# Two transformer layers on one core: one of eight band distances taken from the tokens' difference, and five smaller edits

## The chip, the cores and the metric

The kernel runs on one core of one Trainium2 chip, as one launch. The core has four engines that compute: TensorE (PE; its weight loads are listed apart as PEld), VectorE (DVE), ScalarE (ACT) and GpSimd (POOL). SyncE (SP) issues most of the DMAs. Each engine takes its own queue in order; they meet through semaphores. The metric is the device time of a launch in microseconds (us), the median of several runs, lower is better. Beside it there is one execution taken by the hardware profiler, and all durations below are from that one.

## The reference

Input x has shape (4, 512, 128): four rows of 512 tokens with 128 channels, all in float32. Each of two layers computes `xn = layernorm(x)` and `x = x + attention(xn) + experts(xn)`. Cut to what matters:

```python
# layer 0, attention: 16 heads, 16 displacement channels each, window of 64 tokens
disp = heads(xn @ W_disp); val = heads(xn @ W_val)            # (B, 16, T, 16), (B, 16, T, 8)
strain = windows(disp, 64) - disp[:, :, :, None, :]           # token t-63 .. t, minus token t
bond   = gelu(strain @ W_strain + rel_pos_emb @ W_pos) @ W_bond
damage = sigmoid(gelu(strain @ W_dmg + b_dmg) @ W_dmg_out + b_dmg_out)
weights = softmax(where(causal, bond - 10.0 * damage, -inf))  # over the 64
attention0 = concat(einsum(weights, windows(val, 64))) @ W_cproj
# layer 0, experts: t = rmsnorm(xn) * scale; top 4 of 16 by gate, softmax of their scores, swiglu experts
# layer 1, attention: 16 heads of 8, softmax over all 512 tokens, no mask
# layer 1, experts: router relu(xn @ rw1 + rb1) @ rw2 + rb2, top 2 of 8, softmax of the two,
#                   experts relu(xn @ W1 + b1) @ W2 + b2
```

Strain is linear in the tokens: `(disp[t-d] - disp[t]) @ W_strain` is the same as `(xn[t-d] - xn[t])` projected with `W_disp` and `W_strain` merged. At distance d = 0 the strain is zero for every token.

## The kernel before

**Layer 0** (lines 690 to 994) goes over the four rows. `prepare(b)` normalises a row (`layernorm`, lines 210 to 236: statistics of four tiles, one Sqrt on ScalarE, four normalisations), transposes it to `xnT`, and multiplies it with `merged` (displacement and bond or damage weights in one matrix of 128 x 128 for each of two kinds and two halves of the heads) into `proj` (lines 739 and 740). It also makes the values `valn` and the experts' gate through `routes`.

`band_logits(b)` makes the logits of the 64 distances. A distance is `8 * do + 4 * dq + dd` with do in 0..7, dq in 0..1 and dd in 0..3. For every do, for both kinds (1 is damage, 0 is bond), and for every dd there is one tile `z` of 128 partitions with both dq and both head halves, some 4 x 480 elements: VectorE subtracts two shifted views of `proj` (line 790), ScalarE applies Gelu in place (line 792 for damage in one operation; line 796 for bond in two, since the bias depends on the distance), and TensorE multiplies each quarter with a placing matrix of 32 columns into one of four column strips of a PSUM bank (line 804). Four `z` buffers rotate. Four dd make a bank full, and a Tanh (damage, line 819) or three VectorE operations (bond, lines 822 to 827) read it. After all do, the maxima over the window are subtracted, Exp is applied (line 850, tile `e`) and the row is stored to DRAM (`by_t`, line 851).

Beside this, `gated_experts(b)` runs the row's 16 experts (lines 901 to 923; its PSUM tiles `gbank` come from a pool of three banks), `band_values(b - 1)` multiplies the row before's weights with the values: it loads `f` from `by_t` (line 317), transposes it (line 326), stores it to `by_s` (line 332), loads it back skewed as `wb` (line 344) and multiplies (lines 358 and 362). `begin(b - 1)` then normalises that row for layer 1 and computes its router. `weave` interleaves these generators' steps in the shares that stand beside them.

**Layer 1** (from line 997) weaves `full_attention` (142 steps; products of scores on line 1205, maxima on VectorE on line 1222, Exp on ScalarE on line 1229, weighted values on line 1117) with a second track: the last row's band values, its `begin`, its expert order (`row3`), `experts` for the pairs of the first three rows (`first_experts`) and of the last one, and `results`. An expert block is one weight load `wx` and one gather of rows `xb` by GpSimd (line 581), a turn (lines 604 and 606), a first product (line 637) with Relu (lines 648 and 650), a second one (line 611), and a store of `y` to `ys` (line 619). `results` gathers each token's two rows of `ys` back (`got`, line 581 again) and adds them to x (line 676), `lag` steps after the gather.

What sets the order: each engine's queue is fixed when the program is built. The tile framework's scheduler puts the woven steps in order by priority and by its own estimates of readiness; the placing matmuls, the scores, the maxima and the Exps are raised in priority. `paced` and `behind` tie the experts' products and the results to the steps that are already issued. Where a function (`exp`, `tanh`, `gelu`, `sqrt`) is not in the table that ScalarE holds, a table load goes before it; `Relu` and copies need none.

## Time and profile before

| | us |
|---|---|
| median of three runs | 1317.91 |
| lowest and highest | 1314.45 and 1323.61 |
| the profiled execution's own time | 1310.25 |
| its span, first to last instruction | 1308.1 |

| engine | busy us | share of the span |
|---|---|---|
| TensorE | 1027.7 | 79% |
| VectorE | 1010.7 | 77% |
| ScalarE | 955.3 | 73% |
| GpSimd | 139.1 | 11% |

The shares are averages over two layers of different kind. Layer 0 ends at about 838 us, layer 1 takes the rest. The mean granted clock of TensorE is 0.903 of full speed. A row of busy times gives, for each stretch of time, the busy microseconds of each engine. A row of a group gives the source line, engine, operation, the tiles written and read, the number of instructions, then busy time and the mean of one in ns, then the engine's idle time just before them and what ended it. A line in order of time gives start and duration, and in brackets the idle time before it with its releaser.

### The profile page before, as it was taken

The page shows a single profiled execution, that of the slowest core. Times are in us where ns is not written, and L with a number is a line of the kernel's source. Part 1 is how long each engine was busy: PE and PEld are TensorE (multiplying, and loading weights), DVE is VectorE, ACT ScalarE, POOL GpSimd, SP SyncE. Part 2 cuts the span into 40 slices and gives each one's busy share as a digit, 9 for nine tenths or more (in the row PEclk, how much of TensorE's full clock was granted, in tenths as well). Part 3 has the DMA queues.
Part 4 walks back from the last instruction along what each step waited for, and adds up shares of the span by engine and source line. Part 5 has one row for each costly group of instructions (what it writes and reads, how often), then busy time and mean ns, then how long its engine had stood idle before and what let it go on. Part 6 is the DMA issues. An engine that isn't in the chain of part 4 may idle for free. (4 is left out here: it accounts for less than half of the span.)

```text
span 1308.1 us, 18393 instructions
## 1 busy us (share of the span) xinstructions
PE 1027.7 (79%) x7029; PEld 463.6 (35%) x7029; DVE 1010.7 (77%) x1246; ACT 955.3 (73%) x1154; POOL 139.1 (11%) x165
## 2 busy tenths in 40 slices
PE   5677876778796677897577886739898999978996
PEld 3232333223342132443222342414344545534442
DVE  5999999999988999998999979625355475545552
ACT  5999998999987899898899987224454445534454
POOL 3000000000000000000000000231121123234512
PEclk9898898889998799898788988759999999989999
DMA  7221213347212445311355411154632324532431
GB/s 272 65 85 43 73 55 131 84 117 181 57 46 79 116 105 144 99 57 32 123 131 143 122 51 29 63 164 124 169 93 94 97 66 123 144 104 90 122 112 37
DMA packets 161969, 132.17 MB, mean 101 GB/s; under 512 B 68101, under 2 KB 142266, under 8 KB 160346
## 3 DMA queue, kind: packets, MB, share of 16 engines
q1 hardware_dynamic: 151290, 91.72, 25.7%
q0 software_dynamic: 10304, 38.64, 9.5%
q8 instruction: 56, 0.92, 0.3%
q10 hardware_dynamic: 288, 0.64, 0.1%
q14 instruction: 31, 0.25, 0.1%
HBM read 97.93 MB, written 33.03 MB: 100 GB/s over the span
## 5 line engine op out<-in xcount | busy, mean ns | idle before, releaser
L790 DVE TENSOR_TENSOR z<-proj 128x2044 f32<-128x2044 f32 (+31 forms) x256 | 547.8, 2161 | 14.3 <-PE lbank L804 10.1
L804 PE MATMUL lbank<-z,place 128*32 128x504 f32 (+18 forms) x2048 | 302.5, 669 | 135.2 <-ACT z L796 73.4
L796 ACT ACTIVATE z<-z,posb 128x1024 f32<-128x1024 f32 (+31 forms) x256 | 264.3, 1100 | 24.3 <-DVE z L790 23.6
L792 ACT ACTIVATE z<-z,brep 128x2048 f32<-128x2048 f32 (+31 forms) x128 | 240.8, 1913 | 13.7 <-DVE z L790 11.2
L1229 ACT ACTIVATE ex<-score 128x1024 f32<-128x1024 f32 x128 | 130.4, 1024 | 160.7 <-PE score L1205 160.7
L1222 DVE TENSOR_REDUCE nmax<-score 128x2 f32<-128x1024 f32 x128 | 156.1, 1224 | 84.6 <-PE score L1205 84.2
L804 PEld LDWEIGHTS lbank<-z,place 128*32 128x32 f32 x2048 | 45.3, 115 | 288.9 <-ACT z L796 150.7
L1205 PE MATMUL score<-kpad,qpad 32*128 32x512 f32 x384 | 111.4, 652 | 19.4 <-DVE nmax L1222 14.1
L581 POOL DMA_INDIRECT wx<-pair_weights,which x46 | 43.5, 946 | 663.9 <-PE abank L1097 432.4
L1205 PE MATMUL score<-qa,kpad 32*128 32x512 f32 x384 | 104.1, 654 | 2.9 <-ACT ex L1229 2.8
L893 PE MATMUL accbank<-wT,lin 128*128 128x128 f32 x512 | 84.8, 308 | 23.7 <-DVE lin L891 23.6
L893 PEld LDWEIGHTS accbank<-wT,lin 128*128 128x128 f32 x512 | 71.9, 210 | 75.3 <-DVE lin L891 39.1
L906 PE MATMUL gbank<-tT,wT 128*128 128x512 f32 x128 | 73.3, 656 | 27.1 <-DMA wT<-wT_all 21.2
L648 DVE TENSOR_SCALAR h<-bank,wx 128x128 f32<-128x128 f32 x46 | 16.0, 349 | 77.9 <-ACT h L650 77.9
L913 PE MATMUL gbank<-tT,wT 128*128 128x512 f32 x128 | 69.3, 624 | 4.5 <-ACT glu L909 4.5
L1117 PE MATMUL accbank<-ex,vaug 128*32 128x512 f32 x512 | 71.1, 621 | 0.2 <-ACT ex L1229 0.2
L650 ACT ACTIVATE h<-bank,wx 128x128 f32<-128x128 f32 x138 | 40.7, 365 | 39.2 <-PE bank L637 39.1
L637 PE MATMUL bank<-xbT,wx 128*128 128x128 f32 x368 | 53.9, 291 | 4.3 <-DVE y L618 3.5
L637 PEld LDWEIGHTS bank<-xbT,wx 128*128 128x128 f32 x368 | 47.4, 201 | 24.3 <-issue 15.1
L611 PEld LDWEIGHTS bank<-wx,h 128*128 128x128 f32 x368 | 46.6, 197 | 21.5 <-issue 19.0
L611 PE MATMUL bank<-wx,h 128*128 128x128 f32 x368 | 53.4, 289 | 0.8 <-ACT g L327 0.6
L909 ACT ACTIVATE glu<-gbank,gbt 128x512 f32<-128x512 f32 x64 | 44.2, 690 | 9.0 <-PE gbank L906 6.4
(242 smaller groups left out, 1379.8 us busy)
## 6 DMA issues: line engine op xcount, KB each, us to landing
r<-route SPq DMA_DIRECT2D x64, 256.0 KB
wb<-by_s SPq DMA_DIRECT2D x32, 512.0 KB
wT<-wT_all SPq DMA_DIRECT2D x48, 192.0 KB
by_t<-e SPq DMA_DIRECT2D x8, 1024.0 KB
f<-by_t SPq DMA_DIRECT2D x128, 64.0 KB
by_s<-g SPq DMA_DIRECT2D x16, 512.0 KB
wb<-by_s SPq DMA_DIRECT2D x24, 256.0 KB
by_s<-zero POOLq DMA_DIRECT2D x4, 1024.0 KB, 11.0
```

The source lines that it names most:

```text
L611: mm = nc.tensor.matmul(py[:, 0:C], h[:, c * P:(c + 1) * P], wx[j][:, F1 + c * P:F1 + (c + 1) * P], start=(c == 0), stop=(c == 3),)
L637: mm = nc.tensor.matmul(ph[:, c * P:(c + 1) * P], wx[j][:, c * P:(c + 1) * P], xbT[g][:, j % 2 * P:(j % 2 + 1) * P], start=True, stop=True,)
L790: nc.vector.tensor_tensor(z[:, :, :, 0:n], seen, own, ALU.subtract)
L792: nc.scalar.activation(z[:, :, :, 0:n], z[:, :, :, 0:n], AF.Gelu, bias=b_dmg)
L796: last = nc.scalar.activation(z[:, dq, :, 0:n], z[:, dq, :, 0:n], AF.Gelu, bias=posb[:, j:j + 1])
L804: mm = nc.tensor.matmul(ps[q:q + 32, t0:T], place[:, kind, 3 - dd:35 - dd], z[:, dq, hg, 0:n], start=(dd == 0), stop=(dd == 3),)
L893: nc.tensor.matmul(ya[:, i * P:(i + 1) * P], lin[:, i * P:(i + 1) * P], wT[:, 2, :], start=False, stop=(e == E0 - 1 and i == TPB - 1),)
L906: nc.tensor.matmul(pg, wT[:, 0, :], tT, start=True, stop=True)
L1117: mm = nc.tensor.matmul(av[n][r:r + 32, :], vaug[b % 2][:, i, g * 4 + h, :], ex[n, i][:, h, :], start=(i == 0), stop=(i == TPB - 1),)
L1205: mm = nc.tensor.matmul(ps[:, h - two, :], own[r, i * P:(i + 1) * P], seen[r, :], start=True, stop=True)
L1222: freed.append(nc.vector.tensor_reduce(nmax[n % 2][:, i, two:two + 2, 8:9], ps, AX.X, ALU.max, negate=True))
L1229: freed.append(nc.scalar.activation(ex[n, i][:, two:two + 2, :], ps, AF.Exp, scale=inv))
```

## The change

Six edits:

1. *One of eight distances projected.* For dd = 0 and do over 0, the half of `z` with dq = 0 (distance 8 * do) is no longer a difference of `proj`. VectorE makes `xd`, the difference of the tokens themselves (once, used for both kinds), TensorE multiplies it with `merged` for both head halves into two `gbank` tiles in PSUM, and ScalarE's Gelu reads these and writes `z`. The half with dq = 1 is a difference as before, half as large. `tokens[b]` keeps `xnT`, which now has two buffers.
2. *Distance 0.* Its Gelu has the same value for every token: `alike` holds it for each kind, one column, and the placing matmul reads that column repeated.
3. *Routers' exps.* `exp(x)` is computed as `(1 + tanh(x/2)) / (1 - tanh(x/2))`, with three more small VectorE operations.
4. *Statistics.* `layernorm` is split into `statistics` and `normalise_row`; rows 1 to 3 of layer 0 take their statistics together, with one Sqrt.
5. *Band values.* The last row's first step (its loads of `f`) is issued before layer 1's weave, and eight steps of the first experts go ahead of the rest of that track.
6. *Results.* Those of the first three rows have a lag of 3 in place of 2, and five steps of the last experts go ahead of them. Shares of the weave are set to match.

```diff
-    def layernorm(b, dst, pin=False, rms=False):
+    def statistics(lo, n, pin=False, rms=False):
...
+        return mv, rs
+
+    def normalise_row(b, dst, mv, rs):
...
-        nc.scalar.activation(dst, dst, AF.Exp)
-        nc.vector.tensor_tensor(dst, dst, rank, ALU.mult)
+        nc.scalar.activation(dst, dst, AF.Tanh, scale=0.5)
+        below = small.tile([P, TPB, n], FP, tag=f"below{n}", name="below")
+        nc.vector.tensor_scalar(below, dst, -1.0, 1.0, ALU.mult, ALU.add)
+        nc.vector.reciprocal(below, below)
+        nc.vector.scalar_tensor_tensor(dst, dst, 1.0, rank, ALU.add, ALU.mult)
+        nc.vector.tensor_tensor(dst, dst, below, ALU.mult)
...
+            if b < 2:
+
+                stats.append(statistics(b * TPB, NT - TPB if b else TPB, b > 0, True))
+            mv, rs = stats[-1]
...
-            xnT = prep.tile([C, T], FP, tag="xnT", name="xnT")
+            xnT = prep.tile([C, T], FP, tag="xnT", name="xnT", bufs=2)
...
+                        far = slice(0 if dd else 1, 2)
...
-                        nc.vector.tensor_tensor(z[:, :, :, 0:n], seen, own, ALU.subtract)
+                        if dd:
+                            nc.vector.tensor_tensor(z[:, :, :, 0:n], seen, own, ALU.subtract)
+                        else:
+                            if kind and t0:
+                                xd = ap_.tile([C, T], FP, tag="xd", name="xd", bufs=1)
+                                nc.vector.tensor_tensor(
+                                    xd[:, 0:n], tokens[b][:, 0:n], tokens[b][:, t0:T], ALU.subtract
+                                )
+                            nc.vector.tensor_tensor(
+                                z[:, 1, :, 0:n], proj[:, kind, :, 0:n], proj[:, kind, :, 4 + t0:4 + T], ALU.subtract
+                            )
+                        if not dd and t0:
+                            j = WIN - 1 - t0
+                            for hg in range(2):
+                                pz = ps_g.tile([P, T], FP, tag="g", name="gbank")
+                                nc.tensor.matmul(
+                                    pz[:, 0:n], merged[:, kind, hg, :], xd[:, 0:n], start=True, stop=True
+                                )
+                                nc.scalar.activation(
+                                    z[:, 0, hg, 0:n], pz[:, 0:n], AF.Gelu, bias=b_dmg if kind else posb[:, j:j + 1]
+                                )
                         if kind:
-                            nc.scalar.activation(z[:, :, :, 0:n], z[:, :, :, 0:n], AF.Gelu, bias=b_dmg)
+                            nc.scalar.activation(z[:, far, :, 0:n], z[:, far, :, 0:n], AF.Gelu, bias=b_dmg)
                         else:
-                            for dq in range(2):
+                            for dq in range(far.start, 2):
...
-                                        ps[q:q + 32, t0:T], place[:, kind, 3 - dd:35 - dd], z[:, dq, hg, 0:n],
+                                        ps[q:q + 32, t0:T], place[:, kind, 3 - dd:35 - dd],
+                                        z[:, dq, hg, 0:n] if t0 or dq else alike[:, kind:kind + 1].to_broadcast([P, T]),
...
-    first_experts = experts(early, pq, 3)
...
+    first_experts, last_experts = experts(early, pq, 3), experts(last_row, pq, 3)
+    next(row3)
     weave(
         (full_attention(), 142),
         (after(
-            woven((row3, 32), (first_experts, 36)), first_experts,
-            woven((results(early, 2), 9), (experts(last_row, pq, 3), 34)), results(last_row, 1),
-        ), 32 + 66 + 9 + 34 + 3 + 10),
+            some(first_experts, 8), woven((row3, 31), (first_experts, 30)), first_experts,
+            some(last_experts, 5), woven((results(early, 3), 9), (last_experts, 29)), results(last_row, 1),
+        ), 8 + 61 + 28 + 5 + 38 + 3 + 14),
     )
```

`some(g, n)` takes n steps of a generator.

More of the change, by code (lines that the diff above doesn't have):

```diff
@@ L207, in two_layers @@
     b_dmg = brep[:, 34:35]
-    def layernorm(b, dst, pin=False, rms=False):
-        mv = small.tile([P, TPB, 2], FP, tag="mv", name="mv")
-        for i in range(TPB):
+    def statistics(lo, n, pin=False, rms=False):
+        mv = small.tile([P, n, 2], FP, tag=f"mv{n}", name="mv")
+        for i in range(n):
             st = small.tile([P, 6], FP, tag="st", name="st")
-            ins = nc.vector.bn_stats(st, x1[:, b * TPB + i, :])
+            ins = nc.vector.bn_stats(st, x1[:, lo + i, :])
             if pin and not i:
@@ L220, in layernorm @@
         var = mv[:, :, 1]
-        n = 1 + rms
-        sq = small.tile([P, n, TPB], FP, tag=f"sq{n}", name="sq")
+        sq = small.tile([P, 1 + rms, n], FP, tag=f"sq{n * (1 + rms)}", name="sq")
         nc.vector.tensor_scalar(sq[:, 0], var, EPS, None, ALU.add)
@@ L228, in layernorm @@
         nc.scalar.activation(sq, sq, AF.Sqrt)
-        rs = small.tile([P, n, TPB], FP, tag=f"rs{n}", name="rs")
+        rs = small.tile([P, 1 + rms, n], FP, tag=f"rs{n * (1 + rms)}", name="rs")
         nc.vector.reciprocal(rs, sq)
+        return mv, rs
+    def normalise_row(b, dst, mv, rs):
         for i in range(TPB):
             nc.vector.tensor_scalar(
-                dst[:, i, :], x1[:, b * TPB + i, :], mv[:, i, 0:1], rs[:, 0, i:i + 1],
+                dst[:, i, :], x1[:, b * TPB + i, :], mv[:, i, 0:1], rs[:, i:i + 1],
                 ALU.subtract, ALU.mult,
             )
-        return rs[:, n - 1]
     def transposed(src):
@@ L440, in begin @@
         nc.sync.dma_start(out=rw1, in_=w["L1_ffn_rw1"])
-        layernorm(b, xn)
+        mv, rs = statistics(b * TPB, TPB)
+        normalise_row(b, xn, mv, rs[:, 0])
         nc.sync.dma_start(
@@ L687, in after, with some @@
             yield from p
+    def some(g, n):
+        for _ in range(n):
+            next(g)
+            yield
     with ExitStack() as l0:
@@ L722, in two_layers @@
         nc.scalar.copy(merged.rearrange("p k g n -> p (k g n)"), pm)
-        ready = {}
+        ready, tokens = {}, {}
+        stats = []
         def prepare(b):
             xn = prep.tile([P, TPB, C], FP, tag="xn", name="xn")
-            rr = layernorm(b, xn, b > 0, True)
+            if b < 2:
+                stats.append(statistics(b * TPB, NT - TPB if b else TPB, b > 0, True))
+            mv, rs = stats[-1]
+            own = slice((b - 1) * TPB, b * TPB) if b else slice(0, TPB)
+            normalise_row(b, xn, mv[:, own], rs[:, 0, own])
+            rr = rs[:, 1, own]
             pt = transposed(xn)
-            xnT = prep.tile([C, T], FP, tag="xnT", name="xnT")
+            xnT = prep.tile([C, T], FP, tag="xnT", name="xnT", bufs=2)
             nc.scalar.copy(xnT, pt)
@@ L741, in prepare @@
             ready[b] = [proj]
+            tokens[b] = xnT
             yield
@@ L927, in two_layers @@
             next(preparation)
+        alike = keep.tile([P, 2], FP, name="alike")
+        nc.scalar.activation(alike[:, 1:2], b_dmg, AF.Gelu)
         w_posrep = keep.tile([BD, 8, BD], FP, name="w_posrep")
@@ L938, in two_layers @@
         nc.scalar.copy(posb, pst[:, 0:WIN])
+        nc.scalar.activation(alike[:, 0:1], posb[:, WIN - 1:WIN], AF.Gelu)
         half_b_out = keep.tile([P, 1], FP, name="half_b_out")
@@ L1234, in two_layers @@
     pq = ctx1.enter_context(tc.tile_pool(name="experts", bufs=1))
-    first_experts = experts(early, pq, 3)
-    row3 = after(band_values(B - 1, ready[B - 1][1]), begin(B - 1, chain, "valn"), in_order_of_experts(last_row, pq, pq, "tb"))
+    row3 = after(
+        band_values(B - 1, ready[B - 1][1]), begin(B - 1, chain, "valn"), in_order_of_experts(last_row, pq, pq, "tb")
+    )
+    first_experts, last_experts = experts(early, pq, 3), experts(last_row, pq, 3)
+    next(row3)
     weave(
```

## The prediction

> **What bounds the kernel now.** The profiled execution took 1310.25 us (span 1308.1 us). Busy time by stretches comes first: which engine is full, and where. Columns: stretch, length, busy us (instructions) of PE, PEld, DVE, ACT, POOL, granted TensorE clock, DMA share, GB/s.
>
> ```profile
> 16.50:838.00 821.50, 622.43 (x4094) 257.06 (x4092) 767.87 (x827) 736.33 (x796) 0.22 (x2) 0.89 0.33 91
> 838.00:868.00 30.00, 7.91 (x38) 4.29 (x39) 10.27 (x14) 7.33 (x7) 16.54 (x15) 0.69 0.48 166
> 900.00:1284.00 384.00, 348.38 (x2628) 179.27 (x2632) 202.83 (x340) 188.87 (x314) 98.46 (x104) 0.96 0.40 112
> ...
> 225.00:275.00 50.00, 35.16 (x232) 10.94 (x236) 49.74 (x36) 46.78 (x42) 0.00 (x0) 0.80 0.41 108
> 275.00:325.00 50.00, 39.02 (x410) 17.64 (x405) 49.80 (x42) 47.44 (x52) 0.00 (x0) 0.97 0.61 154
> 325.00:375.00 50.00, 42.00 (x240) 16.71 (x232) 49.28 (x77) 49.21 (x59) 0.00 (x0) 1.00 0.22 60
> 375.00:425.00 50.00, 36.01 (x210) 17.31 (x202) 40.80 (x57) 39.94 (x44) 0.11 (x1) 0.84 0.19 63
> ```
>
> Layer 0, to 838 us, is held by VectorE (767.87 of 821.5), with ScalarE close behind (736.33). The last four lines are one batch row. Its first half has VectorE at 99.54 of 100 us, ScalarE at 94.22. In the second half both are near 90 and TensorE is at 78: there the three wait for each other. Then comes a hole (TensorE 7.91 of 30), then layer 1, which TensorE holds (348 of 384). The costliest groups, per operation:
>
> ```profile
> L790 DVE TENSOR_TENSOR z<-proj 128x2044 f32<-128x2044 f32 (+31 forms) x256 | 547.8, 2161 | 14.3 <-PE lbank L804 10.1 <-ACT proj L740 4.1
> L796 ACT ACTIVATE z<-z,posb 128x1024 f32<-128x1024 f32 (+31 forms) x256 | 264.3, 1100 | 24.3 <-DVE z L790 23.6 <-issue 0.2
> L792 ACT ACTIVATE z<-z,brep 128x2048 f32<-128x2048 f32 (+31 forms) x128 | 240.8, 1913 | 13.7 <-DVE z L790 11.2 <-DVE logits L823 2.1
> L819 ACT ACTIVATE dmg<-lbank,half_b_out 128x512 f32<-128x512 f32 (+7 forms) x32 | 21.2, 663 | 9.8 <-PE lbank L804 9.7
> L827 DVE TENSOR_TENSOR mx<-mx,logits 128x504 f32<-128x504 f32 (+6 forms) x28 | 18.2, 651 | 0.1
> L739 PE MATMUL bank<-xnT,merged 128*128 128x512 f32 x32 | 17.9, 685 | 0.7 <-ACT xnT L732 0.7
> ```
>
> L739 has 16 products in the program and 32 in the trace: each fp32 product is two passes, so it costs 17.9/16 = 1.12 us, not 0.685. Last, the order in time at the hole and at the first gathered results:
>
> ```profile
> 867.09 1.94 PE L326 MATMUL bank<-cst,f 128*128 128x128 f32 x8 [16.84 <-DMA f<-by_t]
> ...
> 1166.38 0.35 DVE L676 SCALAR_TENSOR_TENSOR x<-got,gate,x 128x128 f32<-128x128 f32 x1 [5.83 <-DMA got<-ys,place]
> ...
> 1169.25 1.22 PE L1205 MATMUL score<-kpad,qpad 32*128 32x512 f32 x2 [6.82 <-DVE nmax L1222]
> ...
> 1174.52 0.70 PE L1205 MATMUL score<-kpad,qpad 32*128 32x512 f32 x2
> ```
>
> TensorE's queue stood 16.84 us behind a transpose of the last row's band, although other work was ready. Later one VectorE add waited 5.83 us for gathered rows, the maxima behind it came late, TensorE idled 6.82 us, and then a pass took 1.22 us instead of 0.70.
>
> **Projected distance (dd = 0, seven of eight groups, four rows: 28 times, both kinds).** VectorE: L827 (0.651 us at some 484 elements) and L790 (2.161 at some 1922) give 1.05 ns an element, so 1.15 us for 960 and 0.65 for the tokens' difference. Two full differences (4.32) become 2 x 1.15 + 0.65 = 2.95: -1.37 x 28 = -38. ScalarE: the damage kind's 1.91 becomes 1.10 + 2 x 0.66 (L819 also reads PSUM at that length), the bond kind's 2.20 becomes 2.42: +0.73 x 28 = +20. TensorE: 112 products of 480 columns at 1.12 x 480/512 = 1.05: +117. This is the term that speaks against the change.
>
> New waits: a Gelu that reads PSUM waits for its product; behind it on ScalarE stand the far half's Gelu and the next differences', and TensorE's placing matmuls wait for those. The products share three PSUM banks with the gated experts, and the next tokens' difference waits for the last product that read its single buffer, with VectorE's later differences behind it. The trace of before has nothing like it. Bounds: nothing (each product is issued one or two differences ahead), and about 4 us a row second half (the longest waits of this kind there, PE lbank on z, are 3 to 4 us); I take 1 us a row.
>
> **Distance 0.** Half of each difference goes: VectorE -1.07 x 8 = -8.6, ScalarE -1.0 x 8 = -8. The matmuls stay and read one repeated column; I cost them as before.
>
> **Tables.** The trace has 35 table loads, the changed program 22: Tanh shares a set with Gelu, and with Exp in layer 1, and three rows share one Sqrt. The Trainium skill (ScalarE: Activation LUTs, What ACT_TABLE_LOAD costs) gives 1283 ns plus a drain of 1380 for a switch. The trace has loads of 1283 ns with 0.1 us idle before nine of them, and the Sqrt after the one at 341.98 us starts at 343.27: no drain. By the row 13 loads are -16.7 us, by the page an estimated -34.7; I take the row. The Trainium skill (VectorE: DVE Perf Modes, The TRN2 errata) warns that operations reading SBUF pay a fixed cost each, on ScalarE too, and asks for 512 elements or more, which speaks against cutting one Gelu into three; the new Gelus have about 480, and the 0.66 us already holds that cost. Paid as the page fears, with L796's intercept (1100 - 0.846 x 961 = 0.29 us) once more for 56 extra instructions, ScalarE would get +16 us.
>
> **Routers, statistics.** Three more small VectorE operations in each of eight routers, at about 0.2 us (L264's 0.22): +5, of which +3 in layer 0; shared statistics save about -2.
>
> **Layer 0 by halves.** First half: VectorE 99.5 - 2.1 - 3 x 1.37 = 93.3; ScalarE 94.2 - 2.0 + 2.2 = 94.4; TensorE 74.2 + 3 x 4.2 = 86.8. The bound falls from 99.5 to 94.4; with a less perfect fit I take -3.5. Second half: VectorE 90.1 - 5.5 = 84.6; ScalarE 89.2 + 2.9 - 3 or 4 loads = 88; TensorE 78 + 16.8 = 94.8 at the clock of 0.92 shown, some 88 at full clock. All three meet at 88, so I take -2 from fewer loads, +1 for the new waits: -1. Four rows: 4 x (-4.5) = -18. Bounds: -9 a row if the halves follow their bounds, +4 if the second halves lose 7.
>
> **Last row's handover.** In the changed order, between the transposes of the row maxima and L326's counterpart, three first expert layers, two second ones and four more groups of scores are issued. Each such expert group takes 1.1 us and a score group with its maxima about 4.5 us (870 to 888 us): 5.5 + 18 fills the 16.84, except where an expert's Relu stands behind the row's Exp on ScalarE (until 855.5). The vector clearing on POOL, which waited 7.57 us for the store of the row, now has two expert weight fetches behind it; they are for the fourth block on, after the hole. SP's queue between the store and the first fetches of f is the same. I take -13, bounds -3 and -17.
>
> **Results with lag 3, after five expert steps.** Today's gathers are issued at 1162.5 and used at 1166. A lag of one more step, about 10 us, covers the landing. Gone would be 6.8 idle, about 2 of slow passes after it, 1.1 at 1195 us and 2.4 plus 0.7 at 1213: 13; I take -11 (bounds 0, if another wait takes the place, and -14). The tail: the last experts end three score steps earlier, so more steps run uncovered (3.25 us against 2.2 of TensorE work, +1 each), and the last gathers no longer delay the last row (-1.2): 0.
>
> Sum: -18 - 13 - 11 = -42, to 1268 us of the profiled execution. That lies 7.7 us under the median of 1317.91, so the median goes to **1276 us**.
>
> **Rivals.** (1) *TensorE becomes layer 0's bound, slower than before*: the second halves need 94.8 us of TensorE, and in layer 0 its fullest stretch reached 42.0 of 50 (84%). At 84% they take 113 us: +13 a row, and if the first halves too are held back by ordered queues (86.8/0.84 = 103, +3.8), +67 - 24 = +43: 1361. With the clock of 1.00 this is milder (some 105: +5, then +1): 1318 or less. It decides against the change once layer 0 loses over 24 us. For it: TensorE takes its queue in order. Against: layer 1 runs it at 91%, and its clock of 0.89 rises when it is fuller. 9%. (2) *ScalarE and the waits eat layer 0's gain*, layer 1's stays: -24, 1294. 28%. (3) *Layer 0 follows its bounds*, -36 - 13 - 11 = -60: 1258. 15%. (4) *The edits at the handover only move the hole* (experts wait for Exp, scores for maxima): -18 - 3 - 0 = -21, 1297, or with (2) at zero, no change. 6%. Likeliest, as summed: 42%.
>
> **Range and chances.** 1252 to 1303 leaves out (1), the zero of (4) and the fringe of (3). A difference under 1% (13 us) can't be told from none by three runs that spread over 9. Faster by over 1%: 0.84; within: 0.08; slower: 0.08.
>
> **What would show it.** L790's counterpart with 192 full differences, 64 half ones near 1.15 us, 28 short near 0.65; 112 products near 1.05; 112 PSUM Gelus near 0.66; 22 loads. Layer 0 ending near 820 with ScalarE the fullest in first halves and TensorE at 85 to 90%; no 17 us wait before the last row's transposes; no add waiting 5.8 us for got. I am wrong if ScalarE's waits on the new products are over 1 us each, or VectorE waits for banks: then layer 0 is not shorter.

## The result and the profile after

The changed kernel takes 1362.88 us (median of six runs, 1357.41 to 1370.63) beside 1317.26 (1314.45 to 1323.61) for the kernel before: a ratio of 1.0343, 95% interval 1.0303 to 1.0383. Predicted was 1276 with a range of 1252 to 1303. The direction was wrong. The profiled execution has a span of 1360.3 us, 52.2 more than before: layer 0 ends 29 us later, and layer 1 takes 23 us more. A profile shows one execution, and that of the kernel before took 1310.25 us, under its median: the medians lie 45.6 us apart, so some 7 of the 52 are the choice of the execution.

The work itself is what the prediction said it would be. The groups of the changed kernel (per group: busy us, mean ns of one, then the engine's idle time before them and what ended it):

```profile
L816 DVE TENSOR_TENSOR z<-proj 128x2044 f32<-128x2044 f32 (+11 forms) x192 | 412.1, 2160 | 15.1 <-PE lbank L849 13.6 <-ACT z L841 0.7 <-ACT glu L955 0.7
L849 PE MATMUL lbank<-z,place 128*32 128x487 f32 (+30 forms) x2016 | 297.5, 615 | 57.5 <-ACT z L841 36.9 <-ACT z L837 16.0 <-DVE z L816 2.3
L830 PE MATMUL gbank<-xd,merged 128*128 128x504 f32 (+6 forms) x224 | 112.8, 600 | 3.4 <-DVE xd L820 3.4
L823 DVE TENSOR_TENSOR z<-proj 128x1024 f32<-128x1024 f32 (+7 forms) x64 | 74.2, 1160 | 34.3 <-PE lbank L849 30.0 <-ACT z L841 2.1 <-ACT proj L761 2.1
L833 ACT ACTIVATE z<-gbank,brep 128x504 f32<-128x504 f32 (+6 forms) x56 | 35.3, 663 | 6.8 <-PE gbank L830 6.6
L833 ACT ACTIVATE z<-gbank,posb 128x504 f32<-128x504 f32 (+6 forms) x56 | 35.0, 672 | 3.0 <-PE gbank L830 3.0
L820 DVE TENSOR_TENSOR xd<-xnT 128x504 f32<-128x504 f32 (+6 forms) x28 | 18.3, 652 | 1.3 <-ACT xnT L753 1.1 <-PE gbank L830 0.2
```

192 full differences, 64 half ones at 1.16 us, 28 short ones at 0.65, 112 products (224 passes) at 112.8/112 = 1.01 us, 112 Gelus from PSUM at 0.66 and 0.67. Only one number is new: VectorE stands idle for 30 us before the half differences (L823), because TensorE's placing products have not freed a `z` buffer. ScalarE's waits on the new products, where the prediction looked for trouble, are only 9.6 us in the whole layer.

So layer 0 is not longer because there is more to do. Busy times by stretch (columns as in the first table above), first of the kernel before (its row for layer 0 up to 838 us stands in the prediction), then of the changed one, up to the same 838 us, and in each the stretch do = 3 of the second batch row.

```profile
284.40:304.30 19.90, 13.26 (x142) 5.20 (x142) 19.90 (x16) 19.73 (x19) 0.00 (x0) 1.00 0.54 133
```

```profile
16.50:838.00 821.50, 691.59 (x4195) 288.88 (x4198) 705.16 (x825) 711.08 (x843) 0.22 (x2) 0.93 0.34 91
286.90:324.10 37.20, 27.13 (x242) 14.70 (x231) 21.88 (x23) 24.67 (x30) 0.00 (x0) 0.86 0.66 162
```

Before, do = 3 took 19.9 us with VectorE full. After, it takes 37.2 us, and **no** engine is full: TensorE 27.13, VectorE 21.88, ScalarE 24.67. The same happens in each of the last three rows (19.9, 18.0, 18.5 us before; 37.2 in all three after). The three stretches lose 55 us together. About half of it comes back: do = 4 to 7 of the same rows take 27.5 us less in sum than before. What the engines wait for can be read in order of time (start, duration, engine, line, operation; idle time and its releaser in brackets), still of the changed kernel:

```profile
285.80 1.03 PE L849 MATMUL lbank<-z,place 128*32 128x493 f32 x8 [0.98 <-ACT z L841]
286.65 0.40 PE L365 MATMUL bank<-wb,va 128*32 128x128 f32 x8
...
292.20 1.11 PE L244 MATMUL bank<-cst,avs 128*128 128x128 f32 x4 [4.05 <-ACT avs L374]
293.11 2.06 PE L333 MATMUL bank<-cst,f 128*128 128x128 f32 x8
...
294.96 1.20 PE L952 MATMUL gbank<-tT,wT 128*128 128x512 f32 x2
...
296.00 1.02 PE L959 MATMUL gbank<-tT,wT 128*128 128x512 f32 x2
...
296.86 1.80 PE L830 MATMUL gbank<-xd,merged 128*128 128x488 f32 x4
...
298.82 4.05 PE L849 MATMUL lbank<-z,place 128*32 128x488 f32 x32 [0.17 <-ACT z L833]
...
300.56 1.18 DVE L823 TENSOR_TENSOR z<-proj 128x976 f32<-128x976 f32 x1 [6.62 <-PE lbank L849]
...
310.68 1.12 PE L244 MATMUL bank<-cst,avs 128*128 128x128 f32 x4 [2.27 <-ACT avs L374]
...
317.22 1.80 PE L830 MATMUL gbank<-xd,merged 128*128 128x488 f32 x4
318.96 3.47 PE L849 MATMUL lbank<-z,place 128*32 128x488 f32 x26
```

From 286.83 to 298.82 TensorE issues no placing product. Its queue holds the previous row's band values (L365), their transposes (L244, which wait 4.05 us for a copy that stands behind a Gelu on ScalarE), the transposes of `f` (L333), one expert's two products (L952, L959), and only then the projected products (L830). The four differences that VectorE made ahead wait, with their Gelus done, for the first placing product of the bank, which needs the projected quarter; so VectorE stops for 6.62 us with all four `z` buffers taken. From 302.87 to 318.96 it happens again for the bond kind. In the kernel before, the placing products of dd = 0 needed nothing of TensorE itself, and band values filled the gaps between them.

In layer 1 the hole at the handover is gone. The changed kernel's transposes of the last row's band, which had waited 16.84 us:

```profile
899.76 0.60 PE L333 MATMUL bank<-cst,f 128*128 128x128 f32 x4
901.18 0.66 PE L333 MATMUL bank<-cst,f 128*128 128x128 f32 x4 [0.82 <-DVE y L626]
```

From the row's last do to the first Exp of layer 1 it took 54.6 us before and 40.4 after: 14 us won, where 13 were predicted. But the first Exp comes 14.5 us late (29 less 14) and the last one 53.5 us late: the rest of layer 1 loses 39 us, of which 11 fall among the last twelve Exps (20.0 us before, 31.0 after, from the end of the Exp ahead of them to the end of the last).

Not all of the 39 us is made by layer 1's edits. Here is the stretch from the first Exp to the last, of the kernel before, of the changed one, and of `e1` (below), whose layer 1 is written as before:

```profile
892.58:1296.96 404.38, 365.66 (x2742) 185.04 (x2742) 209.39 (x352) 202.30 (x331) 105.56 (x112) 0.97 0.39 109
907.13:1350.51 443.38, 375.22 (x2744) 186.85 (x2744) 211.05 (x357) 200.29 (x326) 102.98 (x109) 0.94 0.38 102
925.97:1348.59 422.62, 375.42 (x2742) 189.91 (x2742) 209.71 (x354) 202.12 (x331) 105.22 (x112) 0.94 0.38 104
```

In e1 it is 18 us longer than before, at a granted clock of 0.94 in place of 0.97. Five more kernels below with layer 1 written as before (e3, e7, e8, e13, e16) take 408.5 to 416.2 us. So the edits of layer 1 account for some 21 to 35 us of the 39; why a layer 1 written as before takes 4 to 18 us longer beside another layer 0 stays open.

### The profile page after: what moved, and what is told of

The parts are those of the page before. It is cut to its first block, busy times and chain, and to the rows that moved or that the text cites. A ratio compares the mean times of both kernels' runs of the same rounds, so it can differ in the third digit from the quotient of the medians.

```text
span 1360.3 us, 18922 instructions
## 1 busy us (share of the span) xinstructions
PE 1128.0 (83%) x7253; PEld 510.4 (38%) x7253; DVE 973.8 (72%) x1288; ACT 944.9 (69%) x1221; POOL 139.0 (10%) x165
## 5 line engine op out<-in xcount | busy, mean ns | idle before, releaser
L816 DVE TENSOR_TENSOR z<-proj 128x2044 f32<-128x2044 f32 (+11 forms) x192 | 412.1, 2160 | 15.1 <-PE lbank L849 13.6
L849 PE MATMUL lbank<-z,place 128*32 128x487 f32 (+30 forms) x2016 | 297.5, 615 | 57.5 <-ACT z L841 36.9
L841 ACT ACTIVATE z<-z,posb 128x1024 f32<-128x1024 f32 (+13 forms) x224 | 231.4, 1099 | 24.5 <-DVE z L816 16.3
L837 ACT ACTIVATE z<-z,brep 128x1024 f32<-128x1024 f32 (+31 forms) x128 | 213.8, 1708 | 21.8 <-DVE z L816 10.9
L849 PEld LDWEIGHTS lbank<-z,place 128*32 128x32 f32 x2016 | 55.0, 111 | 218.8 <-ACT z L841 90.6
L1255 PE MATMUL score<-kpad,qpad 32*128 32x512 f32 x384 | 112.6, 660 | 23.8 <-DVE nmax L1272 17.8
L830 PE MATMUL gbank<-xd,merged 128*128 128x504 f32 (+6 forms) x224 | 112.8, 600 | 3.4 <-DVE xd L820 3.4
L823 DVE TENSOR_TENSOR z<-proj 128x1024 f32<-128x1024 f32 (+7 forms) x64 | 74.2, 1160 | 34.3 <-PE lbank L849 30.0
L1167 PE MATMUL accbank<-ex,vaug 128*32 128x512 f32 x512 | 74.7, 651 | 0.2 <-ACT ex L1279 0.2
L952 PE MATMUL gbank<-tT,wT 128*128 128x512 f32 x128 | 70.2, 631 | 1.5 <-ACT z L841 1.2
L959 PE MATMUL gbank<-tT,wT 128*128 128x512 f32 x128 | 69.1, 622 | 1.3 <-ACT glu L955 0.8
L658 ACT ACTIVATE h<-bank,wx 128x128 f32<-128x128 f32 x138 | 40.6, 365 | 37.9 <-PE bank L645 28.7
L619 PE MATMUL bank<-wx,h 128*128 128x128 f32 x368 | 56.3, 300 | 2.7 <-DVE y L626 2.7
```

What stands on the lines that cost most here:

```text
L619: mm = nc.tensor.matmul(py[:, 0:C], h[:, c * P:(c + 1) * P], wx[j][:, F1 + c * P:F1 + (c + 1) * P], start=(c == 0), stop=(c == 3),)
L816: nc.vector.tensor_tensor(z[:, :, :, 0:n], seen, own, ALU.subtract)
L823: nc.vector.tensor_tensor(z[:, 1, :, 0:n], proj[:, kind, :, 0:n], proj[:, kind, :, 4 + t0:4 + T], ALU.subtract)
L830: nc.tensor.matmul(pz[:, 0:n], merged[:, kind, hg, :], xd[:, 0:n], start=True, stop=True)
L837: nc.scalar.activation(z[:, far, :, 0:n], z[:, far, :, 0:n], AF.Gelu, bias=b_dmg)
L841: last = nc.scalar.activation(z[:, dq, :, 0:n], z[:, dq, :, 0:n], AF.Gelu, bias=posb[:, j:j + 1])
```

## The experiments

Eighteen kernels ran, in five groups that each shared runs of the kernel before (1310.7 to 1315.6 us, by group). A ratio is to those. A theory's names: P, TensorE has no room for the products; Q, the products stand at a bad place in TensorE's queue.

**Which part costs?** `e1` puts layer 1 back as before. `e2` keeps all but the projection: the full difference for all but distance 0. `e3` does both, so that distance 0, Tanh routers and shared statistics are left. The diff is that of e2; e1 puts the lines of layer 1's weave back as they stand in the change's diff.

```diff
-                        far = slice(0 if dd else 1, 2)
+                        far = slice(0 if t0 else 1, 2)
...
-                        if dd:
+                        if t0:
                             nc.vector.tensor_tensor(z[:, :, :, 0:n], seen, own, ALU.subtract)
                         else:
-                            if kind and t0:
-                                xd = ap_.tile([C, T], FP, tag="xd", name="xd", bufs=1)
...
-                        if not dd and t0:
...
```

> The change with layer 1's second track as before (no eight expert steps ahead, lag 2, old shares); layer 0 as changed. Aligned at the subtraction of the last row's maxima, the changed kernel is 29 us late at the end of layer 0 and loses another 23.5 us in layer 1. If that second loss is made by the new order of layer 1: about 1340 us. If layer 1 is slow for another reason (what layer 0 leaves behind, the clock): about 1363 us, no better than the change.

> The change without the projected distance: dd = 0 is a full difference again, distance 0, tables, statistics and layer 1's new order stay. If the projection makes all of layer 0's loss, layer 0 ends some 29 us earlier and keeps the gains of distance 0 and of fewer tables (10 to 15 us): 1320 us, with no stretch of 37 us at do = 3. If the other edits of layer 0 make the loss: near 1363 us.

> Without the projection and with layer 1 as before: what is left is distance 0, the routers' Tanh and the shared statistics. If the two losses are apart and add up: 1363 - 29 - 12 - 23 = about 1300 us, under the kernel before (1317). If they overlap, or the small edits are worth nothing: 1317 us.

Measured: e1 1355.66, 1.0299 (1.0258 to 1.0339); e2 1339.85, 1.0195 (1.0162 to 1.0228); e3 1325.33, 1.0070 (1.0046 to 1.0095). All three are slower than the first of the two times named for each, and no part wins: the small edits cost 9 us, the projection 20 (changed kernel against e2) to 30 (e1 against e3), layer 1's edits 6 (changed against e1) to 16 (e2 against e3). In e2 and e3 the stretch do = 3 is back at 18.8 to 19.9 us in rows 1 to 3, so that loss belongs to the projection.

**Place or room?** `e4` raises the projected products' priority to that of the placing ones. `e5` leaves them out at do = 3 alone. `e6` issues each one twice.

```diff
-                                nc.tensor.matmul(
-                                    pz[:, 0:n], merged[:, kind, hg, :], xd[:, 0:n], start=True, stop=True
-                                )
+                                with tc.high_priority(offset=4000):
+                                    nc.tensor.matmul(
+                                        pz[:, 0:n], merged[:, kind, hg, :], xd[:, 0:n], start=True, stop=True
+                                    )
```

> The change with the projection's products raised in the scheduler's priority as the placing matmuls are; same work. Theory Q (the products stand too late in TensorE's queue, behind band values that wait for DMA and ScalarE, at do = 3 of rows 1 to 3, 17 to 19 us each): in the new order the damage kind's products at do = 3 stand before the band values, the bond kind's still behind an expert's two: at least a third of the 55 us goes, 1345 us or less. Theory P (TensorE has no room for 117 us more of products, the prediction's first rival): no change, 1363 us.

```diff
-                        far = slice(0 if dd else 1, 2)
+                        full = dd or do == 3
+                        far = slice(0 if full else 1, 2)
...
-                        if dd:
+                        if full:
...
-                        if not dd and t0:
+                        if not full and t0:
```

> The changed kernel, but at do = 3 (16 of the 112 products) both kinds take the full difference as before. Theory Q (at do = 3 of rows 1 to 3 the projected products stand in TensorE's queue behind the pieces of the band values, so the four z buffers fill): those three stretches fall from 37 to about 19 to 20 us, and the time from 1363 to between 1335 and 1345, since some 9 us of each was given back two stretches later. If the same wait only moves to do = 4, that stretch grows to 40 or more. Theory P (TensorE has no room for the products): a seventh of the projection's cost of 23 us goes, 1360, and no single stretch loses more than 3 us.

```diff
                                 nc.tensor.matmul(
                                     pz[:, 0:n], merged[:, kind, hg, :], xd[:, 0:n], start=True, stop=True
                                 )
+                                nc.tensor.matmul(
+                                    pz[:, 0:n], merged[:, kind, hg, :], xd[:, 0:n], start=True, stop=True
+                                )
```

> The changed kernel with each projected product issued twice into the same bank: 112 more products, about 113 us more of TensorE, and no new wait of another engine. Theory P: layer 0 is held by TensorE's work, so rows get longer by most of 28 us each, 1363 to 1440 or more. Theory Q: what costs is when the products are issued, not how much they are; each do has 4 more us of work on an engine that is idle for 5 to 10 us of it, so 1363 to 1375 at most 1390.

e4: 1370.75, 1.0425 (1.0393 to 1.0456), do = 3 still at 34.4, 34.8 and 36.9 us. This spoke against Q, or so it seemed: in its trace the damage kind's products now come early, but the bond kind's still stand behind band values and the experts. e5: 1352.47, 1.0330 (1.0260 to 1.0399). do = 3 falls to 20.8, 20.7 and 17.8 us, but do = 4 rises to 38.7, 38.7 and 38.9: the wait moves to wherever projected products next meet the band values. That is Q's second case; P expected no such stretch. e6: 1416.85, 1.0814 (1.0766 to 1.0861), 62 us over the changed kernel by the ratios, for 118.8 us more of products (231.6 in place of 112.8). This is between the two, and it can't decide: with 112 products more, TensorE is busy 727 of layer 0's first 821.5 us with less of the layer done, so room is short by then whatever held the changed kernel.

**Cheap products.** `e12` makes `xd` and a copy of `merged` bfloat16.

```diff
+        merged16 = lp.tile([C, 2, 2, P], mybir.dt.bfloat16, name="merged16")
+        nc.vector.tensor_copy(merged16, merged)
...
-                                xd = ap_.tile([C, T], FP, tag="xd", name="xd", bufs=1)
+                                xd = ap_.tile([C, T], mybir.dt.bfloat16, tag="xd", name="xd", bufs=1)
...
-                                    pz[:, 0:n], merged[:, kind, hg, :], xd[:, 0:n], start=True, stop=True
+                                    pz[:, 0:n], merged16[:, kind, hg, :], xd[:, 0:n], start=True, stop=True
```

> The changed kernel with the tokens' difference and the merged weights of the projected products in bfloat16 (lower precision of one of eight distances). [...]some 80 us of TensorE's work go; products, waits, banks and the Gelus from PSUM stay. Theory P (in the second halves TensorE's work is what the projection costs, 0.8 us for each us as the doubled products showed): 15 to 20 us of the 23 come back, 1340 to 1348. Theory Q (the cost is the wait for a product behind the band values' pieces): the time stays within 1355 to 1368 and do = 3 stays above 33 us.

```profile
L832 PE MATMUL gbank<-xd,merged 128*128 128x504 bf16 (+6 forms) x112 | 38.9, 381 | 5.3 <-DVE xd L822 4.4 <-ACT lin L963 0.8
```

1353.89, 1.0287 (1.0245 to 1.0330). The products' time falls from 112.8 to 38.9 us, yet only about 7 us come back, and do = 3 stays at 36.3, 32.7 and 36.6. With two thirds of the added TensorE work gone nearly all of the loss is still there, so P is not its main cause. The time fell just under what Q had expected.

**Banks.** The projected products take their PSUM tiles from the pool of three that the experts use. `e14` gives them one bank of their own, the experts two, with the raised priority of e4; `e18` the bank alone.

```diff
-        ps_g = l0.enter_context(tc.tile_pool(name="ps_g", bufs=3, space=PSUM))
+        ps_g = l0.enter_context(tc.tile_pool(name="ps_g", bufs=2, space=PSUM))
+        ps_p = l0.enter_context(tc.tile_pool(name="ps_p", bufs=1, space=PSUM))
...
-                                pz = ps_g.tile([P, T], FP, tag="g", name="gbank")
+                                pz = ps_p.tile([P, T], FP, tag="p", name="pbank")
```

> The changed kernel with the projected products in a PSUM bank of their own (the gated experts keep two of the three) and raised in priority as the placing products are. Theory Q (a product stands in TensorE's queue behind band values and behind experts that hold the shared banks): do = 3 of rows 1 to 3 falls from 37 to 25 us or less, and the time to 1335 to 1348. If the place and the bank don't matter, do = 3 stays above 33 and the time within 1355 to 1372.

> The changed kernel with the projected products in a PSUM bank of their own, without raised priority. If the sharing of banks with the experts is the whole cause: do = 3 near 21 us and 1320 to 1335, as with the priority. If the product also needs its place ahead of the band values: do = 3 at 30 us or more and 1345 to 1365.

e14: 1324.53, 1.0103 (1.0068 to 1.0137); e18: 1328.60, 1.0172 (1.0116 to 1.0228). Some 22 us come back with the bank alone, 32 with both; the two intervals overlap, so what the priority adds is not told apart. do = 3 takes 20.7 and 20.6 us. Here are the same products in order of time in e18 (its line numbers are one higher from the products on):

```profile
283.69 0.57 PE L831 MATMUL pbank<-xd,merged 128*128 128x488 f32 x1
...
286.39 1.08 PE L831 MATMUL pbank<-xd,merged 128*128 128x488 f32 x2
287.36 0.66 PE L244 MATMUL bank<-cst,avs 128*128 128x128 f32 x4
288.24 1.84 PE L850 MATMUL lbank<-z,place 128*32 128x488 f32 x14 [0.22 <-ACT z L834]
290.00 1.08 PE L831 MATMUL pbank<-xd,merged 128*128 128x488 f32 x2
291.02 1.02 PE L850 MATMUL lbank<-z,place 128*32 128x486 f32 x8
291.97 1.09 PE L333 MATMUL bank<-cst,f 128*128 128x128 f32 x8
293.00 1.02 PE L850 MATMUL lbank<-z,place 128*32 128x485 f32 x8
```

Products, placing and band values alternate, and the stretch and the layer fill up (do = 3 of the second row, then layer 0 up to 838 us):

```profile
285.30:305.90 20.60, 17.61 (x116) 5.51 (x107) 19.07 (x16) 19.61 (x23) 0.00 (x0) 1.00 0.55 129
16.50:838.00 821.50, 717.88 (x4337) 295.32 (x4336) 731.99 (x876) 721.53 (x860) 2.42 (x5) 0.95 0.34 91
```

TensorE is busy 717.88 of 821.5 us (87%) where the changed kernel had 691.59 (84%), with the same work to do: there was room. Layer 0's last do ends 5.6 us before that of the kernel before (28.7 after it in the changed kernel; 3.6 after it in e2, without the projection). So the three shared banks are what put the products so late. The sharing acts through their place in the queue more than through waits at run time: in the changed kernel TensorE stood idle for only 3.4 us before the products, and for `xd` (L830 above), and its weight loads for them waited 6.9 us for the experts' Relus that read shared banks. That a product which takes turns with the experts for a bank can't be put ahead of theirs fits e4, where the bond kind's products, raised in priority, still follow an expert's two; no trace shows the choice itself. Two things stay open. The experts now have two banks, and neither e14 nor e18 tells the products' own bank from the experts' smaller share; the kernel before was not run with two. And neither is faster than the kernel before; cheap products in a bank of their own, which would tell whether TensorE's room holds back the rest, were not run.

**Earlier products.** `e15` moves `xd` and both products into a function `project` and calls it two differences earlier, with the products raised, in the shared banks.

```diff
...
+                        if dd == 1 and (do < 7 if not kind else do > 0):
+                            project(do + 1 - kind, 1 - kind)
```

> The changed kernel with the tokens' difference and both products of a group issued two differences earlier (at dd = 1 of the group before) and raised in priority, so that a product is done when its Gelu comes; banks shared as in the changed kernel. Theory L (the cost is the round trip TensorE, ScalarE, TensorE at the start of a group, with VectorE stopped by the four z buffers): do = 3 falls to 20 to 25 us and layer 0 ends 15 to 30 us earlier, 1335 to 1348. Theory P (only TensorE's work counts): the products are as many as before, 1355 to 1368.

1379.89, 1.0538 (1.0491 to 1.0585): theory L is wrong as put, and so are P's numbers. do = 3 stays at 35.6 to 36.9. A product issued earlier also holds a shared bank longer; in the light of e18 that fits, but the early issue in own banks was not tried.

**The small edits alone,** each on the kernel before: `e7` distance 0, `e8` the routers' Tanh, `e13` shared statistics, each with its hunks of the change's diff (and the second buffer of `xnT`); `e16` keeps the Exp and puts operations of the Tanh form's size behind it, four of them, where its expectation says three.

```diff
         nc.scalar.activation(dst, dst, AF.Exp)
+        below = small.tile([P, TPB, n], FP, tag=f"below{n}", name="below")
+        nc.vector.tensor_scalar(below, dst, 1.0, 1.0, ALU.mult, ALU.add)
+        nc.vector.reciprocal(below, below)
+        nc.vector.tensor_scalar(below, below, 0.0, 1.0, ALU.mult, ALU.add)
         nc.vector.tensor_tensor(dst, dst, rank, ALU.mult)
+        nc.vector.tensor_tensor(dst, dst, below, ALU.mult)
```

> The kernel before with the edit of distance 0 alone (half a difference, one repeated column). The prediction's working (VectorE -8.6 us of about 770 in layer 0): 1308 to 1313 beside 1314 to 1317 before. Rival (in the first do of a row VectorE is not what ends the stretch, so nothing is won, and moved instructions may cost some us): 1314 to 1322.

> The kernel before with the routers' exps as Tanh alone: fewer table loads (about 1.28 us each), three more small VectorE operations in each router. The prediction's working: 1300 to 1312 beside 1314 to 1317 before. Rival (table loads lie in ScalarE's slack; the operations and a shifted order cost as much): 1314 to 1325, and then this is where the 9 us came from that the kernel without projection and with layer 1 as before had lost.

> The kernel before with the shared statistics alone. The prediction's working: three table loads or so less and -2 us of VectorE, 1308 to 1315 beside 1312 to 1317. If the three small edits add up (together +9 to +12, distance 0 alone +3, Tanh routers alone +29), it would have to be near -20, 1292 to 1297; if they don't add up, because each one only sets another order of the queues, anything within 20 us of before.

> The kernel before, routers' Exp kept, with three more VectorE operations of the same kind and size behind it (they multiply the result by 1, so the output is as before). By their own cost, 8 routers x 3 x 0.2 us, at most +5: 1313 to 1320. Theory O (a router stands in the chain that starts a row's experts, and a longer one sets another order of the queues, as with the Tanh routers): 1330 to 1345. If it stays below 1320, the Tanh itself, that is where the table loads lie, is what costs.

e7: 1314.37, 1.0027 (0.9992 to 1.0062): no gain, although in its profile VectorE is busy 1002.5 us in place of 1010.7 and ScalarE 947.8 in place of 955.3, as predicted. e13: 1317.64, 1.0006 (0.9980 to 1.0032): no gain. e8: 1341.72, 1.0226 (1.0169 to 1.0282): 30 us slower, with 26 table loads in place of 35. e16: 1329.87, 1.0140 (1.0089 to 1.0192): 18 us slower for four short operations in each router, just under what theory O had put as its least, and far over their own time. They don't add up: the three together (e3) cost 9 us. Two of ScalarE's waits from 200 to 860 us (us in total, times, longest), first in e8, then the same two in the kernel before:

```profile
ACT lin L932 <- PE accbank L910: 19.9, 10, 4.6
ACT glu L926 <- DVE lin L908: 15.9, 6, 5.4
```

```profile
ACT lin L915 <- PE accbank L893: 2.0, 4, 0.8
ACT glu L909 <- DVE lin L891: 2.3, 2, 2.0
```

The experts' steps meet the band's at other places of the queues, because the router, from which a row's experts start, is some operations longer when the schedule is made. That the schedule's order is the whole of the cost of e8 and e16 is argued, not shown.

**Layer 1's edits alone,** on the kernel before: `e9` the handover, `e10` the results with lag 3 and five steps of the last experts ahead (the diffs of both, in this order); `e17` handover and distance 0. `e19` is e14 with the results as before, that is, with e9's weave.

```diff
+    next(row3)
...
-            woven((row3, 32), (first_experts, 36)), first_experts,
+            some(first_experts, 8), woven((row3, 31), (first_experts, 30)), first_experts,
             woven((results(early, 2), 9), (experts(last_row, pq, 3), 34)), results(last_row, 1),
```

```diff
             woven((row3, 32), (first_experts, 36)), first_experts,
-            woven((results(early, 2), 9), (experts(last_row, pq, 3), 34)), results(last_row, 1),
+            some(last_experts, 5), woven((results(early, 3), 9), (last_experts, 29)), results(last_row, 1),
```

> The kernel before with the handover edit alone (first step of the last row's band values before the weave, eight steps of the first experts ahead, lag 2 and the rest as before). The prediction's working: -13, 1300 to 1304 beside 1312 to 1317. Theory G (won at the handover, given back in layer 1 because the band value's loads and the experts' steps now meet the scores at other places): the first Exp comes 12 to 15 us earlier and the last one 0 to 5 us earlier or later, 1310 to 1325.

> The kernel before with the results edit alone (lag 3 for the first three rows' results, five steps of the last experts ahead of them). The prediction's working: -11, 1302 to 1306 beside 1312 to 1317. Theory R (the adds still wait for the gathers, and with the last experts done earlier the last row's results stand on VectorE ahead of the last scores' operands): the adds' waits stay at 25 us or more, the last twelve Exps take 30 us in place of 20, and the time is 1320 to 1328.

> The kernel before with the handover edit and distance 0, nothing else. Alone they gave -3 and +4. If such edits add up, 1312 to 1320. If the handover's early gain of 12 to 15 us is kept with another order in layer 1, 1300 to 1306.

> The changed kernel with own bank and raised priority, and the results as before (lag 2, no five steps ahead). The results edit alone cost 8 to 10: 1312 to 1318 beside 1311 to 1316 before. If it cost more here, where the last twelve Exps took 28 us: 1303 to 1309, faster than before.

e9: 1312.94, 0.9981 (0.9955 to 1.0006). The first Exp comes 11.6 us earlier, at 881.0, and the last one 8.7 us later: theory G's shape, though the last Exp comes later still than it said. Three stretches from the first Exp to the last, of the kernel before and of e9:

```profile
892.60:1024.50 131.90, 119.45 (x973) 59.50 (x974) 65.22 (x99) 66.84 (x105) 20.79 (x22) 0.96 0.45 123
1024.50:1156.80 132.30, 127.39 (x912) 68.94 (x913) 74.43 (x139) 66.66 (x117) 32.14 (x35) 0.97 0.41 112
1156.80:1295.00 138.20, 117.02 (x851) 56.42 (x855) 68.65 (x113) 66.85 (x107) 51.26 (x54) 0.96 0.32 93
```

```profile
881.00:1014.00 133.00, 114.88 (x987) 56.70 (x988) 65.32 (x100) 65.01 (x102) 18.99 (x21) 0.97 0.50 134
1014.00:1154.50 140.50, 130.23 (x900) 69.14 (x901) 73.69 (x137) 67.19 (x116) 30.33 (x33) 0.95 0.39 102
1154.50:1302.60 148.10, 121.08 (x855) 57.71 (x855) 69.40 (x113) 66.66 (x108) 52.23 (x55) 0.94 0.30 88
```

TensorE's work in them is the same (363.86 and 366.19 us), its idle time grows from 38.5 to 55.4, by some 6 us in each third. Part of this is the choice of the executions: the profiled one of e9 took 1319.07 us, beside a median of 1312.94, and that of the kernel before 1310.25, beside 1315.62 in this group, some 11 us between them. The medians are the firmer ground: some 12 to 14 us are won at the hole, but e9 is only 2.5 us faster than the kernel before (5.9 to -0.8 by its interval), and e17 below no faster than e7. So most of what the hole gave is lost again later in layer 1. That it goes in small waits all over the layer rests on this pair of executions; which waits was not settled.

e10: 1323.78, 1.0059 (1.0034 to 1.0085), 8 us slower. The adds' waits for gathered rows after 870 us (in total, times, longest), of the kernel before, of e10 and of the changed kernel:

```profile
DVE x L676 <- DMA got<-ys,place: 27.8, 15, 8.2
DVE x L676 <- DMA got<-ys,place: 23.0, 13, 3.2
DVE x L684 <- DMA got<-ys,place: 30.7, 13, 7.4
```

In e10 the last twelve Exps take 23.0 us in place of 20.0: theory R has the time right, but its two signs only in small. They show in full where handover and results edit come together. The end of the changed kernel:

```profile
1331.86 0.74 DVE L684 SCALAR_TENSOR_TENSOR x<-got,gate,x 128x128 f32<-128x128 f32 x2 [7.35 <-DMA got<-ys,place]
...
1335.89 0.68 DVE L1158 TENSOR_TENSOR qa<-abank,qpad 128x512 f32<-128x512 f32 x1
...
1336.72 2.09 PE L1255 MATMUL score<-qa,kpad 32*128 32x512 f32 x8 [4.79 <-DVE qa L1158]
```

And that of e19:

```profile
1277.62 0.69 DVE L1160 TENSOR_TENSOR qa<-abank,qpad 128x512 f32<-128x512 f32 x1 [1.54 <-PE abank L1105]
1288.38 0.35 DVE L684 SCALAR_TENSOR_TENSOR x<-got,gate,x 128x128 f32<-128x128 f32 x1 [6.42 <-DMA got<-ys,place]
```

In the changed kernel the last row's adds (L684) wait 7.35 us for their rows, and the last scores' operand `qa` stands behind them on VectorE; the last twelve Exps take 31.0 us. In e19 `qa` comes first and the adds wait after it, when VectorE has little else to do: 19.7 us.

e17: 1313.32, 1.0021 (0.9991 to 1.0051), no gain either. e19: 1305.69 (1300.61 to 1316.64) beside 1310.68 (1305.44 to 1317.01), 0.9963 (0.9933 to 0.9994): 18 us less than e14 for the results edit alone, and the only kernel here whose interval lies below 1, by 0.4%. So bank, priority and results edit together answer for 50 us by the ratios, all that the changed kernel had lost; what stays away is the gain.

## Why the prediction was wrong

*The costs of the operations* were right: 1.16 us for the half difference (1.15), 0.65 for the short one (0.65), 1.01 for a product (1.05), 0.66 for a Gelu from PSUM (0.66). VectorE's busy time fell by 36.9 us, TensorE's rose by 100.3, ScalarE's fell by 10.4.

*Layer 0, -18 predicted, +29 measured.* The step that failed is the term of the new waits, "1 us a row", with bounds of nothing and 4: do = 3 alone took 17.3, 19.2 and 18.7 us more in the last three rows, and after what came back these rows are 13.5, 9.9 and 3.7 us longer. The lower bound rested on "each product is issued one or two differences ahead", the upper on the longest waits of the trace before. In the queue the products stood behind other work for 12 and 16 us in which no placing product ran, in one stretch of each of three rows. The prediction noted that they share three banks with the gated experts, and put no price on it; a bank of their own (e18) took back 22 us of the projection's 20 to 30. With own bank and raised priority (e14) layer 0 ends 6.9 us before that of the kernel before, so somewhat over a third of the -18 is there to be had, the small edits' own cost included. Of its signs of being wrong the first stayed away (ScalarE's 13 waits on the new products are 9.6 us, 0.7 each), and the second came in another form: VectorE waited 30 us, for `z` buffers.

*Rival (1)*, TensorE becomes the bound, had the sign, and its 1361 lies beside the 1362.88 measured; but that is a coincidence: it had +67 us in layer 0 and -24 in layer 1, where +29 and +23 were measured, and its mechanism isn't what held this kernel. TensorE at 84% was taken as full; e14 and e18 run it at 87 to 88% in a shorter layer, and cutting the products to a third (e12) gave 7 us. Whether it holds with twice the products (e6) is open.

*Handover, -13 predicted.* The wait went as predicted (-14), the time did not follow (e9: 0.998, interval up to 1.0006). The working asked what fills the hole, not what is then late in the rest of the layer; rival (4) came nearest, but the hole did not move to another place; most of what it gave was lost again over the rest of layer 1.

*Results, -11 predicted, +8 alone and +18 beside the handover.* The step that failed: a lag of three steps was said to cover the landing. The adds still waited 30.7 us for rows in the changed kernel (27.8 before) and 23.0 in e10. Of e10's 8 us, 3 lie among the last twelve Exps; where the rest lies stays open.

*Tail, 0 predicted, +11.* The prediction counted three more uncovered steps and took the last gathers out of the way. It didn't ask which instruction stands behind the adds on VectorE once they come earlier: `qa`.

*Small edits.* Priced by their own operations at a few us, with 13 table loads less for ScalarE. Alone they gave no gain, no gain and +30. Nine loads less did not help e8; that another order of the queues is what counted is argued.

*Slips in the working.* The projection adds 84 instructions on ScalarE (28 times 2 for damage and 1 for bond), not 56, so its estimate of +16 us would have been +24; ScalarE's busy time fell by 10.4, so neither shows. The 34.7 us for 13 loads with a drain is 34.6. And the 1.22 us "instead of 0.70" are two passes each, not one. None of them changes the forecast.

## What to carry to other kernels

When an engine that only consumed in a chain becomes a producer at its head (here TensorE, ScalarE, TensorE), the first question is what stands ahead of the new product in that engine's queue, and which buffers it takes turns for; give it a bank of its own before judging it. A wait filled at one place is won only if something downstream is no longer late, so name what would end last afterwards. And in a kernel whose queues a scheduler orders, an edit worth some 5 us of work can move the time by 20 or 30, as it seems through the order alone: run each edit by itself.

## What the runs showed of the hardware

A product of 128 x 128 weights with some 480 columns took 1.01 us in float32, as two passes, and 38.9/112 = 0.35 us in bfloat16, as one pass. In layer 0's first 821.5 us the granted clock was 0.89 at 622 us of TensorE work (before), 0.93 at 692 (changed) and 0.95 at 718 (e18). That it goes with TensorE's fill is not a rule: e3, at 643 of 829 us, had 0.86.
